# A graph layer's message stage: order written out by hand, more groups in flight, statistics by pairs of banks

## The chip, the core and the metric

The kernel runs on one core of one Trainium2 chip. The core's engines work side by side and meet through semaphores: PE (TensorE, the matrix unit, with its weight loads shown apart as PEld), DVE (VectorE), ACT (ScalarE), POOL (GpSimd) and SP (SyncE, which here only issues DMAs). PSUM, the memory that matmuls write to, has 8 banks of 512 floats in each of 128 partitions. The metric is the device time of one execution in microseconds (us). The time before is the median of three runs, 5669.56 us (5662.26 to 5670.88).

## The reference

One layer of a graph network over 12,500 nodes with 96 features and 412,500 edges, which come sorted by their destination `dst` and carry four attributes each:

```python
def _mlp(h, W, b, gamma, beta):
    h = relu(h @ W + b)
    return gamma * (h - mean(h, 0)) * rsqrt(var(h, 0) + EPS) + beta
node_feat = _mlp(x, W_node, ...)
edge_feat = _mlp(edge_attr, W_edge, ...)
message   = _mlp(concatenate([x[src], x[dst], edge_feat]), W_msg, ...)
out = layernorm(x + segment_sum(message, dst) + node_feat)
```

The normalisation in `_mlp` runs over all rows, so the edge part needs the statistics of relu(edge MLP) over all edges before a single message can be made, and the message part needs the statistics of all messages before the end.

## The kernel before, in words

**Tiling.** 128 edges make a tile, four tiles a *group* (`GT`, `GE` = 512 edges), four groups a *block* (`BG`). There are 806 groups in 202 blocks. Because edges are sorted by destination, a group touches a window of at most 30 nodes (`WN`), which begins at a node number held in `base`.

**Stage 1, tables (L136).** `p_tab` = x @ W_msg's first part (needed by source) and `q_tab` = x @ W_msg's second part (needed by destination) go to DRAM. `table()` fills PSUM tiles `pt` (4 buffers) and copies them out by ACT and DVE in turn.

**Stage 2, nodes (L202) and edge statistics (L234).** For each block `edge_norm()` runs three matmuls of 10 rows by 512 columns (L249) into a tile of three PSUM banks (two buffers), one relu on ACT over all three (L252, 128x1536) and three `bn_stats` on DVE (L254). From the result come `w_e`, the scaled edge weights, and `bias`.

**POOL beside it.** POOL gathers rows of `p_tab` by source with indirect DMAs, one per tile, four per group (L289). While stage 2 runs, it gathers the first 26 blocks (`SPILL`), here called *early*, into `stage` (two buffers); SP writes them to DRAM (`spill`, L303) and they are read back when their turn comes (`pb`, L404). After the early blocks POOL fills a ring of 30 groups (`RING`) with the groups that follow; from then on a group's slot must be freed before the next one is gathered. The order of SP and POOL up to here is written out by hand (`manual_schedule`).

**Stage 3, messages (L342 to L440).** The 176 other blocks, here called *late*, are taken in turn, with the 26 early ones spread evenly between them. For each block `load()` has SP fetch the edge attributes (L346), the window offsets (L347) and, after a load of four window bases to DVE's and SP's registers (L349), four windows of `q_tab` into `rhs` (L353, two slots). `prepare()` makes the four products `pr`, 6 rows by 512 columns each, into one tile of four banks (L362); ACT takes the relu of 96 rows of it (L364, 96x2048), DVE the zero test of the 30 others (L365, 30x2048), which is a one-hot of the destination in the window. Both make `left`. Then for each group `message()` runs four matmuls `z` = left x rhs (L371: edge part, destination part and bias together), DVE makes a second one-hot `h[.., 97:127]` (L373) and adds the gathered rows (`hs` = z + pg, L377), and ACT takes the relu into `h` (L378). One group later `reduce()` runs four matmuls `pa` = h transposed times [h | one-hot] (L386), and DVE adds them to the window of `agg` (L389, the segment sum) and to `gram` (L390, the messages' moments). `hs` is the last reader of a ring slot: POOL's gathers of the group 30 further on wait for it. In this stage the program's scheduler sets the order on each engine. PSUM: pr 4 banks, z 2 and pa 2.

**Stage 4, end (L598).** The messages' normalisation, a product per node tile, and the layer norm.


Of the kernel before, what the change touches and what calls it, by code (L numbers as in the profile page):

```python
# [22 lines left out]
P = 128  # L23
# [27 lines left out]
WN = 30  # L51
KR = C + WN + 1

SPILL = 26 * BG
RING = 30
J = 8


# [12 lines left out]
def gnn(ctx, tc, t):  # L71
# [61 lines left out]
        return s[:, 0:1], s[:, 1:2]  # L133


    def table(out, w, work, ps, queues):  # L136

        rows = out.rearrange("(p b) f -> p b f", b=NB)
        for c in range(0, NB, CH):
            r = work.tile([P, CH, C], F32, name="trow", bufs=3)  # L140
            for j, i in enumerate(range(0, CH, NBK)):
                n = min(NBK, CH - i)
                pt = ps.tile([P, NBK, C], F32, name="pt", bufs=4)
                for g in range(n):
                    k = COL[c + i + g]
                    nc.tensor.matmul(pt[:, g, :], xp[:, k:k + P], w, start=True, stop=True)  # L146
                if j % 2:
                    nc.scalar.activation(r[:, i:i + n, :], pt[:, :n, :], AF.Copy)  # L148
                else:
                    nc.vector.tensor_copy(r[:, i:i + n, :], pt[:, :n, :])  # L150
            queues[c // CH % len(queues)].dma_start(rows[:, c:c + CH, :], r)
            yield

    with tc.tile_pool(name="win_w", bufs=1) as work, tc.tile_pool(name="win_ps", bufs=2, space=PSUM) as ps:
        for _ in table(p_tab, w_msg[:, 0, :], work, ps, (nc.sync, nc.scalar)):
            pass

    nc.sync.dma_start(vec, t["vecs"])
# [75 lines left out]
    def edge_norm():  # L234

        with tc.tile_pool(name="es", bufs=2) as work, tc.tile_pool(name="es1", bufs=1) as one, \
                tc.tile_pool(name="es_ps", bufs=2, space=PSUM) as ps:
            stats = one.tile([P, NS, NBL, 6], F32, name="estats")
            for b in range(NBL):
                if b % J == 0:  # L240
                    yield
                    ea = work.tile([P, J, GE], F32, name="ea")
                    n = min(J, NBL - b)
                    for i in range(NS):
                        nc.sync.dma_start(ea[Q * i:Q * i + 2 * EK, :n, :],
                                          t["ea"][EK * i:EK * (i + 2), b:b + n, :])
                pr = ps.tile([P, NS, GE], F32, name="pr")
                for i in range(NS):
                    nc.tensor.matmul(pr[:, i, :], wide[Q * i:Q * i + 2 * EK, :],  # L249
                                     ea[Q * i:Q * i + 2 * EK, b % J, :], start=True, stop=True)  # L250
                r = work.tile([P, NS, GE], F32, name="r")
                nc.scalar.activation(r, pr, AF.Relu)  # L252
                for i in range(NS):
                    nc.vector.bn_stats(stats[:, i, b, :], r[:, i, :])  # L254

            part = one.tile([P, NS, 2], F32, name="part")
            square = one.tile([P, NS], F32, name="square")
# [27 lines left out]
    def fast(ring):  # L285
# [21 lines left out]
        store = blocks()  # L307
        with tc.manual_schedule(engines={ET.SP, ET.Pool}):
            with tc.tile_pool(name="tab_w", bufs=1) as work, tc.tile_pool(name="tab_ps", bufs=2, space=PSUM) as ps:
                for i, _ in enumerate(table(q_tab, w_msg[:, 1, :], work, ps, (nc.sync,))):  # L310
                    if i in (3, 6):
                        next(store)
            next(store)
# [9 lines left out]
                pass  # L323
            got = {g: ahead_of(g) for g in range(SPILL, SPILL + RING)}

        with tc.tile_pool(name="fix", bufs=1) as fix, tc.tile_pool(name="msg", bufs=2) as work, \
                tc.tile_pool(name="msg_ps", bufs=2, space=PSUM) as ps:
            gram = fix.tile([C + 1, C + 1], F32, name="gram")
            nc.vector.memset(gram, 0.0)
            rhs = fix.tile([P, 2, BG, C], F32, name="rhs")  # L330
            nc.vector.tensor_copy(rhs[:C], w_e[:, None, None, :].to_broadcast([C, 2, BG, C]))
            for i in range(2):
                for k in range(BG):
                    nc.sync.dma_start(rhs[KR - 1:KR, i, k, :], bias)
            left = [fix.tile([P, BG, GE], F32, name=f"left{i}") for i in range(2)]
            for x in left:
                nc.vector.memset(x[C:], 1.0)
            hb = [fix.tile([P, GT, P], F32, name=f"h{i}") for i in range(4)]
            for x in hb:
                nc.vector.memset(x[:, :, C:C + 1], 1.0)  # L340

            def load(s, b):  # L342

                n = min(BG, NG - b * BG)
                ea = work.tile([P, GE], F32, name="ea")
                nc.sync.dma_start(ea, t["eaq"][:, b, :])  # L346
                nc.sync.dma_start(ea[EK:P:Q, :], rel_d[:, b * BG * GE:(b + 1) * BG * GE]  # L347
                                  .rearrange("o (g e) -> (o g) e", g=BG))
                _, val = nc.values_load_multi_w_load_instructions(  # L349
                    base[:, b * BG:(b + 1) * BG], engines=[ET.DVE, ET.SP], min_val=0, max_val=N - 1,  # L350
                    skip_runtime_bounds_check_because="they are nodes' numbers")
                for i in range(n):
                    nc.sync.dma_start(rhs[C:C + WN, s % 2, i, :], q_tab[bass.ds(val[i], WN), :])  # L353
                return ea, val

            def prepare(s, b, ea):

                n = min(BG, NG - b * BG)
                x = left[s % 2]
                pr = ps.tile([C + WN, BG, GE], F32, name="pr", bufs=1)  # L360
                for i in range(n):
                    nc.tensor.matmul(pr[:, i, :], we[Q * i:Q * i + EK + 1, :],  # L362
                                     ea[Q * i:Q * i + EK + 1, :], start=True, stop=True)
                nc.scalar.activation(x[:C, :n, :], pr[:C, :n, :], AF.Relu)  # L364
                nc.vector.tensor_scalar(x[C:C + WN, :n, :], pr[C:, :n, :], 0.0, None, op0=OP.is_equal)  # L365

            def message(s, g, h, pg):
                n = min(GT, NT - g * GT)
                z = ps.tile([P, GT, C], F32, name="z")
                for i in range(n):  # L370
                    nc.tensor.matmul(z[:, i, :], left[s % 2][:KR, g % BG, i * P:(i + 1) * P],  # L371
                                     rhs[:KR, s % 2, g % BG, :], start=True, stop=True)
                nc.vector.tensor_tensor(  # L373
                    h[:, :, C + 1:C + 1 + WN], rel[:, g, :].unsqueeze(2).to_broadcast([P, GT, WN]),
                    iota[:, None, :].to_broadcast([P, GT, WN]), op=OP.is_equal)
# [1 line left out]
                nc.vector.tensor_add(hs[:, :n, :], z[:, :n, :], pg[:, :n, :])  # L377
                nc.scalar.activation(h[:, :n, :C], hs[:, :n, :], AF.Relu)  # L378

            def reduce(g, h, val):  # L380

                n = min(GT, NT - g * GT)
                pa = ps.tile([C + 1, P], F32, name="pa")
                for i in range(n):
                    r = min(P, E - (g * GT + i) * P)
                    nc.tensor.matmul(pa[:, :C + 1 + WN], h[:r, i, :C + 1], h[:r, i, :C + 1 + WN],  # L386
                                     start=i == 0, stop=i == n - 1)
                to = agg[:, bass.ds(val, WN)]
                nc.vector.tensor_tensor(to, pa[:, C + 1:C + 1 + WN], to, op=OP.add)  # L389
                nc.vector.tensor_add(gram, pa[:, :C + 1], gram)  # L390


            early, late = list(range(SPILL // BG)), list(range(SPILL // BG, NBL))
            order = []
            for i, b in enumerate(late):
                order.append(b)
                while early and (SPILL // BG - len(early)) * len(late) < i * (SPILL // BG):
                    order.append(early.pop(0))
            order += early

            def fetch(b):
                if b * BG < SPILL:
                    back = work.tile([P, BG, GT, C], F32, name="pb")
                    nc.sync.dma_start(back, spill[b].rearrange("p g (a c) -> p g a c", a=GT))  # L404
                    for i in range(BG):
                        got[b * BG + i] = back[:, i, :, :]

            ea, val = load(0, order[0])
            prepare(0, order[0], ea)
            fetch(order[0])  # L410
            last, n, ahead = None, 0, SPILL + RING
            for s, b in enumerate(order):
                more = s + 1 < len(order)
                if more:
                    ea, then = load(s + 1, order[s + 1])
                    fetch(order[s + 1])
                for g in range(b * BG, min((b + 1) * BG, NG)):
                    if g % BG == 1 and more:
                        prepare(s + 1, order[s + 1], ea)
                    h = hb[n % len(hb)]  # L420
                    n += 1
                    message(s, g, h, got.pop(g))
                    if last:
                        reduce(*last)
                    last = g, h, val[g % BG]
                    if g >= SPILL and ahead < NG:
                        got[ahead] = ahead_of(ahead)
                        ahead += 1
                val = then
            reduce(*last)  # L430

            d = fix.tile([C, C], F32, name="d")
            s = fix.tile([C, 3], F32, name="s")
# [234 lines left out]
```

## Time and profile before

| what | value |
|---|---|
| median of three runs | 5669.56 us |
| the profiled execution: its time, its span | 5713.74 us, 5712.0 us |
| mean granted TensorE clock in it | 0.656 of full speed |
| first and last `hs` (L377) in it | 1246 us, 5646.5 us |
| ring filled for the first time (POOL idle from there to 1247) | 1160 us |
| POOL's last gather begins at about | 5571 us |
| POOL gathers | 3223, of which 416 early ones |

The profile is one execution. A row of the groups reads: line, engine, operation, out<-in with shapes, count | busy us in all, mean ns of one | idle us of the engine just before these instructions, and what ended most of it ("issue" means nothing that the profile shows). A timeline row reads: start in us, duration in us, engine, line, operation, count of instructions merged, and in brackets the idle time before it and what ended that. A row of stretches gives each engine's busy us and count in a stretch of the span, and the granted clock as a share of full speed (PEclk). "x8" for four matmuls in f32 is right: each is recorded as two passes.

### The profile page before, as it was taken

The numbers are of one execution on the slowest core, as the hardware profiler recorded it, in microseconds if no ns is written. First come the engines' busy times: TensorE is split into PE (matmuls) and PEld (weight loads), VectorE is DVE, ScalarE is ACT, GpSimd is POOL, SyncE is SP. The second block draws the span as 40 slices with busy tenths as digits, with TensorE's granted clock in tenths as the row PEclk, the third lists the DMA queues.
The fourth block names the chain that finished last, engine by engine and source line by source line (L and its number), as shares of the span: only waits on it lengthen the run. The fifth ranks groups of instructions, "written<-read, shape, count | busy, mean of one in ns | idle before, by whom it ended". The sixth has DMA issues, their size and how long they took to land. (4 is left out here: it accounts for less than half of the span.)

```text
span 5712.0 us, 52958 instructions
## 1 busy us (share of the span) xinstructions
PE 3507.9 (61%) x16561; PEld 2613.4 (46%) x16561; DVE 1830.5 (32%) x4227; ACT 1126.2 (20%) x1304; POOL 3070.7 (54%) x3231
## 2 busy tenths in 40 slices
PE   3445666146666666766667566676566666665768
PEld 3331111024545455555555455455455555554547
DVE  1134555142323223232222232232322222322326
ACT  0113444021111111111111111111111111111113
POOL 2254444725555565555565555655555655556550
PEclk9955555557776666566666766666666666666667
DMA  3232323212222222222222222222222222222212
GB/s 117 73 97 56 70 63 68 47 42 51 52 52 49 46 50 52 50 52 49 52 46 51 50 51 49 47 52 49 51 50 52 46 50 52 49 52 46 50 44 82
DMA packets 190423, 315.48 MB, mean 55 GB/s; under 512 B 95817, under 2 KB 96201, under 8 KB 189128
## 3 DMA queue, kind: packets, MB, share of 16 engines
q0 software_dynamic: 103136, 158.62, 13.2%
q1 hardware_dynamic: 83502, 141.01, 8.9%
q10 hardware_dynamic: 3496, 12.36, 0.7%
q8 instruction: 137, 2.24, 0.2%
q14 instruction: 152, 1.25, 0.1%
HBM read 270.34 MB, written 41.37 MB: 55 GB/s over the span
## 5 line engine op out<-in xcount | busy, mean ns | idle before, releaser
L289 POOL DMA_INDIRECT pg<-p_tab,src x2807 | 2670.2, 951 | 1884.8 <-issue 787.5
L371 PE MATMUL z<-rhs,left 127*128 127x96 f32 x6446 | 1330.3, 350 | 706.3 <-issue 385.0
L371 PEld LDWEIGHTS z<-rhs,left 127*128 127x128 f32 x6446 | 1181.7, 261 | 1158.2 <-issue 684.0
L386 PE MATMUL pa<-h 128*97 128x127 f32 x6446 | 1236.4, 355 | 656.2 <-issue 351.7
L386 PEld LDWEIGHTS pa<-h 128*97 128x97 f32 x6446 | 1077.7, 230 | 719.8 <-issue 377.2
L378 ACT ACTIVATE h<-hs 128x384 f32<-128x384 f32 x806 | 419.5, 521 | 3094.3 <-DVE hs L377 1528.7
L389 DVE TENSOR_TENSOR agg<-pa,agg 97x30 f32 x806 | 150.4, 187 | 1978.1 <-PE z L371 752.6
L377 DVE TENSOR_TENSOR hs<-z,pg 128x384 f32<-128x384 f32 x702 | 390.2, 556 | 1054.7 <-issue 471.4
L289 POOL DMA_INDIRECT stage<-p_tab,src x416 | 399.6, 961 | 608.1 <-DMA spill<-stage 428.3
L362 PE MATMUL pr<-ea,we 6*126 6x512 f32 x1612 | 601.4, 841 | 157.4 <-issue 102.5
L249 PE MATMUL pr<-ea,wide 10*128 10x512 f32 x1212 | 406.6, 1107 | 409.2 <-ACT r L252 264.8
L254 DVE BATCH_NORM_STATS2 estats<-r 128x6 f32<-128x512 f32 x606 | 372.1, 680 | 442.6 <-ACT r L252 287.2
L364 ACT ACTIVATE left<-pr 96x2048 f32<-96x2048 f32 x202 | 376.3, 1863 | 549.9 <-remote 260.7
L365 DVE TENSOR_SCALAR left<-pr 30x2048 f32<-30x2048 f32 x202 | 462.9, 2292 | 43.8 <-ACT left L364 37.6
L249 PEld LDWEIGHTS pr<-ea,wide 10*128 10x128 f32 x1212 | 114.5, 307 | 700.0 <-ACT r L252 484.4
L252 ACT ACTIVATE r<-pr 128x1536 f32<-128x1536 f32 x202 | 292.2, 1451 | 592.9 <-remote 384.4
L362 PEld LDWEIGHTS pr<-ea,we 6*126 6x126 f32 x1612 | 150.6, 232 | 226.0 <-issue 150.3
L373 DVE TENSOR_TENSOR h<-rel,iota 128x120 f32<-128x120 f32 x806 | 204.9, 275 | 2.4 <-issue 0.4
L390 DVE TENSOR_TENSOR gram<-pa,gram 97x97 f32<-97x97 f32 x806 | 201.8, 250 | 0.3 <-DVE agg L389 0.3
L146 PE MATMUL pt<-w_msg,xp 96*128 96x96 f32 x392 | 85.6, 423 | 139.2 <-ACT trow L148 131.4
L146 PEld LDWEIGHTS pt<-w_msg,xp 96*128 96x128 f32 x392 | 84.1, 332 | 140.5 <-ACT trow L148 132.2
L223 PE MATMUL py<-center,xp 96*128 96x96 f32 x196 | 43.1, 423 | 60.5 <-DVE y0s L227 37.5
(95 smaller groups left out, 443.5 us busy)
## 6 DMA issues: line engine op xcount, KB each, us to landing
ea<-in_eaq SPq DMA_DIRECT2D x202, 256.0 KB
pg<-p_tab,src POOLq DMA_INDIRECT x2807
spill<-stage SPq DMA_DIRECT2D x26, 768.0 KB
pb<-spill SPq DMA_DIRECT2D x26, 768.0 KB
rhs<-q_tab SPq DMA_DIRECT2D x806, 11.2 KB
ea<-in_ea SPq DMA_DIRECT2D x75, 160.0 KB
stage<-p_tab,src POOLq DMA_INDIRECT x416
q_tab<-trow SPq DMA_DIRECT2D x7, 672.0 KB
```

The source lines that it names most:

```text
L249: nc.tensor.matmul(pr[:, i, :], wide[Q * i:Q * i + 2 * EK, :], ea[Q * i:Q * i + 2 * EK, b % J, :], start=True, stop=True)
L252: nc.scalar.activation(r, pr, AF.Relu)
L254: nc.vector.bn_stats(stats[:, i, b, :], r[:, i, :])
L289: nc.gpsimd.indirect_dma_start(out=pg[:, i, :], out_offset=None, in_=p_tab[:, :], in_offset=bass.IndirectOffsetOnAxis(ap=src[:, k:k + 1], ...
L362: nc.tensor.matmul(pr[:, i, :], we[Q * i:Q * i + EK + 1, :], ea[Q * i:Q * i + EK + 1, :], start=True, stop=True)
L364: nc.scalar.activation(x[:C, :n, :], pr[:C, :n, :], AF.Relu)
L365: nc.vector.tensor_scalar(x[C:C + WN, :n, :], pr[C:, :n, :], 0.0, None, op0=OP.is_equal)
L371: nc.tensor.matmul(z[:, i, :], left[s % 2][:KR, g % BG, i * P:(i + 1) * P], rhs[:KR, s % 2, g % BG, :], start=True, stop=True)
L373: nc.vector.tensor_tensor(h[:, :, C + 1:C + 1 + WN], rel[:, g, :].unsqueeze(2).to_broadcast([P, GT, WN]), iota[:, None, :].to_broadcast([P ...
L377: nc.vector.tensor_add(hs[:, :n, :], z[:, :n, :], pg[:, :n, :])
L378: nc.scalar.activation(h[:, :n, :C], hs[:, :n, :], AF.Relu)
L386: nc.tensor.matmul(pa[:, :C + 1 + WN], h[:r, i, :C + 1], h[:r, i, :C + 1 + WN], start=i == 0, stop=i == n - 1)
```

## The change

Five things change.

1. `SPILL` goes from 26 to 34 blocks: eight more blocks are gathered early, written out and read back.
2. The statistics take PSUM in pairs of banks (four buffers of two instead of two of three): 303 relus of 128x1024 instead of 202 of 128x1536; the matmuls and `bn_stats` are as many as before.
3. The message stage is cut to single groups and its order is written out by hand on all five engines. Step k issues, where they exist: the relu and zero test of group k+3, `z` of k+2, one-hot, `hs` and relu of k, `pa` of k-1, the product `pr` of k+5, the adds of k-3, then the gather into the freed slot. On each engine this is the order of its own instructions: PE runs z(k+2), pa(k-1), pr(k+5); ACT the relu of k+3, then that of k; DVE the zero test of k+3, one-hot and hs of k, the adds of k-3.
4. PSUM is split anew: pr two tiles of one bank, z three, pa three. `left` becomes 8 buffers of one group (before: 2 of four groups), `h` 6 buffers (4), `rhs` 3 slots (2), `ea` 3 (2). A block's loads are issued two blocks ahead instead of one. The 12 rows of `bias` in `rhs` were 8. The bases are loaded to SP's registers in `load` and to DVE's before a block's first add.
5. `table()` gets 8 PSUM buffers for `q_tab` (4 before; `p_tab` stays at 4).

```diff
-SPILL = 26 * BG
+SPILL = 34 * BG
 RING = 30
+LEAD, SKEW = 5, 3
+LB, HB, RB = 8, 6, 3
...
-                pt = ps.tile([P, NBK, C], F32, name="pt", bufs=4)
+                pt = ps.tile([P, NBK, C], F32, name="pt", bufs=bufs)
...
-                tc.tile_pool(name="es_ps", bufs=2, space=PSUM) as ps:
+                tc.tile_pool(name="es_ps", bufs=4, space=PSUM) as ps:
...
-                pr = ps.tile([P, NS, GE], F32, name="pr")
                 for i in range(NS):
-                    nc.tensor.matmul(pr[:, i, :], wide[Q * i:Q * i + 2 * EK, :],
+                    k = NS * b + i
+                    if k % 2 == 0:
+                        pr = ps.tile([P, 2, GE], F32, name="pr")
+                    nc.tensor.matmul(pr[:, k % 2, :], wide[Q * i:Q * i + 2 * EK, :],
                                      ea[Q * i:Q * i + 2 * EK, b % J, :], start=True, stop=True)
-                r = work.tile([P, NS, GE], F32, name="r")
-                nc.scalar.activation(r, pr, AF.Relu)
-                for i in range(NS):
-                    nc.vector.bn_stats(stats[:, i, b, :], r[:, i, :])
+                    if k % 2:
+                        r = work.tile([P, 2, GE], F32, name="r", bufs=4)
+                        nc.scalar.activation(r, pr, AF.Relu)
+                        for o in (1, 0):
+                            nc.vector.bn_stats(stats[:, (k - o) % NS, (k - o) // NS, :], r[:, 1 - o, :])
...
-                for i, _ in enumerate(table(q_tab, w_msg[:, 1, :], work, ps, (nc.sync,))):
+                for i, _ in enumerate(table(q_tab, w_msg[:, 1, :], work, ps, (nc.sync,), 8)):
...
-                tc.tile_pool(name="msg_ps", bufs=2, space=PSUM) as ps:
+                tc.tile_pool(name="msg_ps", bufs=3, space=PSUM) as ps:
...
-            left = [fix.tile([P, BG, GE], F32, name=f"left{i}") for i in range(2)]
+            left = [fix.tile([P, GE], F32, name=f"left{i}") for i in range(LB)]
...
-            hb = [fix.tile([P, GT, P], F32, name=f"h{i}") for i in range(4)]
+            hb = [fix.tile([P, GT, P], F32, name=f"h{i}") for i in range(HB)]
...
+            def edges(k):
+                s, g = steps[k]
+                prs[k] = ps.tile([C + WN, GE], F32, name="pr", bufs=2)
+                i = Q * (g % BG)
+                nc.tensor.matmul(prs[k], we[i:i + EK + 1, :], eas[s][i:i + EK + 1, :], start=True, stop=True)
+
+            def prepare(k):
+                pr, x = prs.pop(k), left[k % LB]
+                nc.scalar.activation(x[:C], pr[:C], AF.Relu)
+                nc.vector.tensor_scalar(x[C:C + WN], pr[C:], 0.0, None, op0=OP.is_equal)
+
+            def linear(k):
+                s, g = steps[k]
+                n = min(GT, NT - g * GT)
+                zs[k] = ps.tile([P, GT, C], F32, name="z")
                 for i in range(n):
-                    nc.tensor.matmul(z[:, i, :], left[s % 2][:KR, g % BG, i * P:(i + 1) * P],
-                                     rhs[:KR, s % 2, g % BG, :], start=True, stop=True)
+                    nc.tensor.matmul(zs[k][:, i, :], left[k % LB][:KR, i * P:(i + 1) * P],
+                                     rhs[:KR, s % RB, g % BG, :], start=True, stop=True)
...
+            with tc.manual_schedule(engines={ET.SP, ET.Pool, ET.PE, ET.DVE, ET.Activation}):
+                for k in range(-LEAD, n + SKEW):
+                    b = k + LEAD
+                    if b == 0:
+                        load(0)
+                        fetch(0)
+                        load(1)
+                    if 0 <= k < n and (k == 0 or steps[k][0] != steps[k - 1][0]):
+                        s = steps[k][0]
+                        if s + 2 < len(order):
+                            load(s + 2)
+                        if s + 1 < len(order):
+                            fetch(s + 1)
+                    if 0 <= k + LEAD - 2 < n:
+                        prepare(k + LEAD - 2)
+                    if 0 <= k + 2 < n:
+                        linear(k + 2)
+                    if 0 <= k < n:
+                        message(k)
+                    if 0 <= k - 1 < n:
+                        sums(k - 1)
+                    if k + LEAD < n:
+                        edges(k + LEAD)
+                    if k - SKEW >= 0:
+                        add(k - SKEW)
+                    if 0 <= k < n and steps[k][1] >= SPILL and ahead < NG:
+                        got[ahead] = ahead_of(ahead)
+                        ahead += 1
```

`message(k)` keeps its one-hot, `hs` and relu; `sums(k)` and `add(k)` are the two halves of the old `reduce()`.

## The prediction

> **What bounds the kernel now.** I read the page first: shares of busy time, the clock, the costly groups.
>
> ```profile
> PE 3507.9 (61%) x16561; PEld 2613.4 (46%) x16561; DVE 1830.5 (32%) x4227; ACT 1126.2 (20%) x1304; POOL 3070.7 (54%) x3231
> ...
> L289 POOL DMA_INDIRECT pg<-p_tab,src x2807 | 2670.2, 951 | 1884.8 <-issue 787.5
> L371 PE MATMUL z<-rhs,left 127*128 127x96 f32 x6446 | 1330.3, 350 | 706.3 <-issue 385.0
> ...
> L389 DVE TENSOR_TENSOR agg<-pa,agg 97x30 f32 x806 | 150.4, 187 | 1978.1 <-PE z L371 752.6
> ```
>
> No engine is full. The message stage lasts from 1246 to 5646.5 us (first and last hs) and 77% of the span; its longest queue is POOL's, 2687 gathers at 0.95 us with 0.30 us of issue between two, 1.25 x 2687 = 3359 us. What POOL waits for in the other thousand us is read from its own waits on the tile pg, between 1300 and 5400 us (duration, window, count of waits; then what ended them, with us and count):
>
> ```profile
> L289 POOL DMA_INDIRECT pg<-p_tab,src x2552: 941/947/1197, 1302.3 to 5398.8; - x197
>   issue: 711.5, 2260
>   DVE h L373: 553.5, 78
>   DVE gram L390: 294.8, 92
> ```
>
> With hs (84.5 us, 28 waits) that is some 198 waits of 4.75 us: a ring slot comes free when hs has read it. So DVE holds POOL, and DVE waits for PE. Why is PE late at 61%? The timeline of one burst answers it (start, duration, engine, in brackets the idle time before):
>
> ```profile
> 2619.15 2.01 PE L386 MATMUL pa<-h 128*97 128x127 f32 x8 [2.53 <-issue]
> 2621.09 2.08 PE L362 MATMUL pr<-ea,we 6*126 6x512 f32 x6
> ...
> 2625.02 0.32 PE L371 MATMUL z<-rhs,left 127*128 127x96 f32 x1 [0.90 <-issue]
> 2626.45 0.32 PE L371 MATMUL z<-rhs,left 127*128 127x96 f32 x1 [1.11 <-issue]
> 2626.57 0.94 POOL L289 DMA_INDIRECT pg<-p_tab,src  x1 [0.30 <-issue]
> ...
> 2630.73 0.19 DVE L389 TENSOR_TENSOR agg<-pa,agg 97x30 f32 x1 [11.87 <-PE z L371]
> 2631.44 0.56 DVE L377 TENSOR_TENSOR hs<-z,pg 128x384 f32<-128x384 f32 x1 [0.35 <-issue]
> ...
> 2632.26 1.20 POOL L289 DMA_INDIRECT pg<-p_tab,src  x1 [4.76 <-DVE h L373]
> ```
>
> While POOL gathers back to back, PE starts well and then crawls at one instruction per 1.1 to 1.4 us, waiting for nothing the profile names ("issue"); the DVE add has stood for 11.87 us for sums run at 2619. POOL runs out of slots at 2627.5, and about 3 us later everything is released at once: add 2630.73, hs 2631.44, next gather 2632.26. I call this the jam. The stretches give its price:
>
> ```profile
> core 0: us, PE busy (x) PEld busy (x) DVE busy (x) ACT busy (x) POOL busy (x), PEclk, DMA share, GB/s
> ...
> 1180.00:1205.00 25.00, 19.99 (x60) 6.22 (x60) 21.20 (x35) 17.19 (x12) 0.00 (x0) 0.50 0.10 36
> 2656.20:2680.60 24.40, 13.97 (x72) 11.52 (x72) 6.51 (x17) 3.74 (x5) 15.39 (x16) 0.64 0.21 46
> 2680.60:2691.20 10.60, 9.38 (x53) 8.53 (x54) 6.54 (x17) 3.74 (x5) 0.00 (x0) 0.68 0.25 65
> ```
>
> A late block (four groups, 16 gathers: 20 us, and one stop of 4.75) takes about 24.6 us, 6.15 per group; the early block after it, same work but no gathers, 10.6. The first row belongs to the statistics: PE is busy 80% of the time with 10-row matmuls, and the granted clock stays at 0.50.
>
> **The change part by part**, against the profiled execution (span 5712.0, its time 5713.74; the median of the runs is 0.9923 of that).
>
> **A. Eight more blocks early (26 to 34).** They leave the message stage as late blocks and come back as early ones: 8 x (24.6 - 10.6) = -112 us. Their 128 gathers go ahead of the ring in POOL's queue: 128 x 1.25 = +160. POOL stood idle from 1160 (ring full) to 1247 (first slot free), so 87 us of slack take part of it, but the statistics are themselves jammed while POOL gathers: an iteration of 12 PE instructions takes 16.8 us under gathers (ACT's relu at 1024.94 and again at 1041.74) and 1.86 us free, and after POOL stops PE needs 15 to 20 us to run freely (1160 to 1175-1180). So the front ends between +73 (all slack used) and about +145 later; I take +120, as the statistics' tail still comes behind POOL's end. A is +8; -40 to +33. SP writes 8 more blocks to DRAM and reads them back, 768 KB each; the reads lie a block ahead, beside 10 us of work at 65 GB/s: 0.
>
> **B. The written order: restart after a stop.** DVE's step now opens with the zero test of group k+3, which waits for ACT's relu of that group's product; hs, the one that frees the slot, is behind both. After the flush the path is relu of 96x512 (0.68, from the rows of L364 at 1.86 for 2048 and the 96x512 relu of the node stage at 0.68), zero test of 512 (0.70, from 2.29 for 2048 and 1.23 for 1024), one-hot 0.28, hs 0.56, POOL's release 0.26: 2.5 us where 2630.73 to 2632.26 shows 1.5. The adds that stood ahead of hs move three groups back (-0.4, counted in the 1.5). Behind the waiting zero test stand one-hot, hs and the adds of older groups, for hs POOL. So +1.0 to 1.1 us on some 200 stops: +220 at most; 0 if PE, which works meanwhile, gives it back later. No row shows such a return, but a late block's cycle is set mostly by POOL's 20 us; I take +50. More groups in flight may lengthen a burst; that is rival 1.
>
> **C. The written order: PE's clock.** Before, a block's four products pr (6 rows) ran together, x2 and x6, and z and pa ran in long dense rows. Now one pr of 512 columns stands alone between each four z and four pa. Warm, a group costs PE 0.89 (z, 2692.98) + 0.87 (pa, 2689.66) + 1.05 (pr, 2688.09) = 2.8 us; cold, about 1.8 + 1.94 + 2.06 (2906.34) = 5.8 us. From the row at 1180, a 6-row product like the 10-row ones does not raise the clock, and it fills 2.06 of 5.8 us, so that once cold a group is 64% dense: in the trace no stretch of 3.4 us with under 0.8 dense work is followed by the full clock. So the early blocks, where nothing but PE and the chain limits, take from 4 x 2.8 = 11.2 to 4 x 5.8 = 23.2 us instead of 10.6: 34 x (0.6 to 12.6) = +20 to +428. I take halfway, 17.2 us, +224, since a full clock once granted holds on through stretches at 0.8 busy, and some early blocks will begin warm. Late blocks: 23.2 us of cold PE work lie within a cycle of 24.7, but only where the jam lets them run: in B's bound.
>
> The Trainium skill ("TensorE: Matmul & The Clock Gate", the section on the HAM clock gate) has the clock rise after about 3.4 us of sustained matmul work and says nothing of narrow rows. By it the denser order would stay warm and C would be +20 instead of +224; the row at 1180 (80% busy, 0.50) speaks against that, and the measurement decides.
>
> **D. The rest, at nothing.** Statistics by pairs: 303 relus of 1024 at about 1.04 (between L252's 1.45 for 1536 and half of L364's 1.86) = 315 us instead of 293, on ACT that is idle for most of the stage; the count of matmuls (1212) and of bn_stats (606) stays; POOL's gathers set the pace, and without them bn_stats at 0.68 does: bounds -15 to +20. The q table with 8 buffers, 7 loops beside POOL's first gathers: -10 to 0. Four more bias DMAs at 0.6 us of SP issue, once: 0 to +3. DVE's own load of block bases moves from the block's load to its first add: same count. ACT issues 806 relus for 202: 806 x 0.68 = 548 for 376, at 20% busy; DVE goes from 1.84 to 1.97 us a group beside 5 or more.
>
> Sum: 8 + 50 + 224 = +282, 5996 profiled, x 0.9923 = **5950 us**. With every term low: -40 + 0 + 20 - 25 = -45, about 5625; every term high: 33 + 220 + 428 + 23 = +704, 6370.
>
> **Rivals.**
> 1. *Faster: longer bursts.* With z and pa three deep, eight left and six h, more groups' hs could be ready at a flush, so that POOL gathers more than four groups before it stops. The late group then costs 5.0 + 4.75/n instead of 6.19 (n = 4; measured 6.15). Against A + C = +232 on 640 groups it decides from n = 6 (0.40 x 640 = -253); n = 8 gives -380 + 232 = -148, 5520 us. For it: the flush at 2630.73 frees two hs in 1.1 us, as many as z had banks. Against: the jam starts some 9 us into a burst whatever is in flight, and DVE's order is now held by a relu and a zero test per group.
> 2. *Jam gone*: PE never falls behind, POOL sets the time: ring full at about 1350 (1160 + 160 + 30), 640 x 5.0 = 3200, 34 x 10.6 = 360, drain and end 145: 5055, 5016 us. Against: the statistics jam under gathers too, with quite another order.
> 3. *Slower still*: cold nearly everywhere and B in full: +430 to +704, 6100 to 6370. For it: mean clock already only 0.656.
> 4. *The change moves nothing*: the terms cancel, within 0.2% (11 us, about what a measurement of this kernel can tell): needs C near +20 and B near 0 at once.
>
> **How the numbers follow.** Forecast (+120 to +430, 5790 to 6100) 0.55; slower by 12 to 120 us 0.10; rival 3 0.12; rival 4 0.03; rival 1 0.15; rival 2 0.05. Faster 0.20, same 0.03, slower 0.77. Range 5520 to 6300: leaves out rival 2, about half of rival 1 and a third of rival 3, under 0.2; the forecast's own is 5790 to 6100.
>
> **What would show it.** A: last early gather and full ring later by about 160 us, first hs at 1350 to 1390; above 1400 the statistics cost more. B: the idle time before a burst's first gather 5.5 to 6 us instead of 4.75, its waits mostly ended by DVE's hs, and still about one stop per four groups; fewer than 110 stops would be rival 1. C: early blocks of 13 to 22 us and a mean clock under 0.62; 11 us and a clock above 0.68 would make C wrong. DVE's zero test should carry the long waits, ended by ACT. The prediction fails most likely if bursts grow beyond four groups.

## The result and the profile after

The changed kernel takes 5887.79 us (median; 5864.74 to 5895.30) against 5668.34 us before: a ratio of 1.0382, 95% interval [1.0351, 1.0413], 219 us slower. The forecast was 5950 us, 282 us slower. The profiled execution has a span of 5893.6 us (5712.0 before) and a mean clock of 0.648 (0.656). The execution profiled before took 5713.74 us, 0.8% more than the median of its runs, so the two traces differ by 182 us and not by 219.

The page of the changed kernel, engines and costly groups:

```profile
PE 4325.3 (73%) x16561; PEld 2924.7 (50%) x16561; DVE 1963.7 (33%) x4839; ACT 1213.1 (21%) x2009; POOL 3059.0 (52%) x3231
...
L294 POOL DMA_INDIRECT pg<-p_tab,src x2679 | 2540.3, 948 | 2031.5 <-DVE gram L435 1254.6
...
L393 DVE TENSOR_SCALAR left<-pr 30x512 f32<-30x512 f32 x806 | 561.5, 697 | 3232.7 <-ACT left L392 2422.3
...
L387 PE MATMUL pr<-ea,we 6*126 6x512 f32 x1612 | 1270.3, 875 | 146.9 <-issue 71.9
...
L434 DVE TENSOR_TENSOR agg<-pa,agg 97x30 f32 x806 | 144.1, 179 | 1.6 <-PE pa L422 1.6
```

The wait that stood before DVE's add (1978 us) now stands before the zero test, L393: 3233 us, put down to ACT, whose relu reads PE's product. PE is busy 817 us longer with the same count of instructions, and 669 us of that is the product pr (601 before, 1270 now): before, the four products of a block, on four different sets of rows, ran in about the time of two; now each stands alone.

POOL's waits on pg between 1300 and 5400 us:

```profile
L294 POOL DMA_INDIRECT pg<-p_tab,src x2380: 938/944/1935, 1299.7 to 5398.8; - x199
its engine sat idle before it (us, times) until:
  DVE gram L435: 1161.1, 169
  issue: 648.0, 2112
```

169 waits of 6.9 us, where there were 198 of 4.7 (the prediction's 4.75; these waits include the long ones over early blocks). `gram` is named because it starts 0.01 us after `hs` ends; the slot is freed by `hs`. One jam and its stop, in the timeline:

```profile
2619.59 1.12 PE L387 MATMUL pr<-ea,we 6*126 6x512 f32 x2
...
2630.82 0.94 POOL L294 DMA_INDIRECT pg<-p_tab,src  x1 [0.30 <-issue]
2631.16 0.32 PE L400 MATMUL z<-rhs,left 127*128 127x96 f32 x1 [1.56 <-issue]
...
2634.73 0.59 ACT L392 ACTIVATE left<-pr 96x512 f32<-96x512 f32 x1 [12.69 <-remote]
2635.36 0.70 DVE L393 TENSOR_SCALAR left<-pr 30x512 f32<-30x512 f32 x1 [13.67 <-ACT left L392]
2636.08 0.28 DVE L407 TENSOR_TENSOR h<-rel,iota 128x120 f32<-128x120 f32 x1
...
2636.40 0.56 DVE L411 TENSOR_TENSOR hs<-z,pg 128x384 f32<-128x384 f32 x1
...
2637.22 0.94 POOL L294 DMA_INDIRECT pg<-p_tab,src  x1 [5.46 <-DVE gram L435]
```

The product that PE ran at 2619.59 reaches ACT at 2634.73, 3 us after POOL's last gather ends (2631.76): the jam is as before. From there to POOL's next gather the path is the predicted one, relu, zero test, one-hot, hs: 2.49 us instead of 1.53.

An early block in three places, and the late block before the first of them, as stretches:

```profile
core 0: us, PE busy (x) PEld busy (x) DVE busy (x) ACT busy (x) POOL busy (x), PEclk, DMA share, GB/s
2689.40:2713.80 24.40, 16.79 (x74) 11.55 (x73) 7.20 (x20) 4.12 (x8) 15.10 (x17) 0.71 0.20 46
2713.80:2728.00 14.20, 14.20 (x67) 10.50 (x66) 7.20 (x20) 4.35 (x8) 2.19 (x3) 0.70 0.11 22
3395.10:3409.90 14.80, 14.80 (x47) 9.75 (x47) 7.23 (x21) 4.24 (x8) 0.00 (x0) 0.50 0.08 22
3532.50:3543.80 11.30, 11.30 (x67) 8.55 (x66) 7.25 (x21) 4.24 (x8) 2.18 (x3) 0.90 0.13 28
```

In an early block PE is busy without a gap, and the time goes by the clock: 11.3 us at 0.90, 14.8 at 0.50. Taking the time between the first hs of a block and that of the next, the 34 early blocks mean 14.1 us (10.6 before; correlation with the granted clock -0.77, before -0.01). Between 1400 and 5400 us, where POOL gathers, a late block that follows an early one means 22.8 (19.3 before), and the other late blocks 25.09 (25.04 before).

**POOL's ledger**, from the two traces, closes on the 182 us between the spans:

| | before | after | difference |
|---|---|---|---|
| first ring gather starts at | 1010 | 1151 | +141 |
| wait at the first full ring | 87 | 0 | -87 |
| ring gathers at 1.25 us | 2807 | 2679 | -160 |
| stops after 1400 us, in all | 974 in 202 | 1231 in 189 | +257 |
| of these, 2 to 8 us long (over no early block) | 161 of 3.66 | 149 of 5.11 | (+172) |
| longer ones, each over an early block | 24 of 14.8 | 31 of 14.8 | (+105) |
| shorter ones | 30 in 17 | 10 in 9 | (-20) |
| last gather to the end of the span | 149 | 172 | +23 |

That is +174; 8 us are in smaller pieces. The last gather starts at 5563 us before (not at 5571) and at 5722 after. The front is no loss. The stops are: +172 us in those that a burst of gathers between two late groups ends with, which are 1.45 us longer each. The stops over early blocks are as long as before, 14.8 us, although the early blocks themselves take 3.5 us more; there are only seven more of them, as eight more blocks are early. Below, stops of 2 to 8 us are counted up to 5550 us, which makes 142 of 5.10 in the changed kernel.

### The profile page after: what moved, and what is told of

The parts are those of the page before. It is cut to its first block, busy times and chain, and to the rows that moved or that the text cites. A ratio compares the mean times of both kernels' runs of the same rounds, so it can differ in the third digit from the quotient of the medians.

```text
span 5893.6 us, 53933 instructions
## 1 busy us (share of the span) xinstructions
PE 4325.3 (73%) x16561; PEld 2924.7 (50%) x16561; DVE 1963.7 (33%) x4839; ACT 1213.1 (21%) x2009; POOL 3059.0 (52%) x3231
## 3 DMA queue, kind: packets, MB, share of 16 engines
q0 software_dynamic: 103136, 158.62, 12.7%
## 5 line engine op out<-in xcount | busy, mean ns | idle before, releaser
L294 POOL DMA_INDIRECT pg<-p_tab,src x2679 | 2540.3, 948 | 2031.5 <-DVE gram L435 1254.6
L393 DVE TENSOR_SCALAR left<-pr 30x512 f32<-30x512 f32 x806 | 561.5, 697 | 3232.7 <-ACT left L392 2422.3
L422 PE MATMUL pa<-h 128*97 128x127 f32 x6446 | 1330.5, 362 | 375.5 <-issue 374.6
L387 PE MATMUL pr<-ea,we 6*126 6x512 f32 x1612 | 1270.3, 875 | 146.9 <-issue 71.9
L422 PEld LDWEIGHTS pa<-h 128*97 128x97 f32 x6446 | 1137.4, 236 | 475.7 <-issue 475.3
L392 ACT ACTIVATE left<-pr 96x512 f32<-96x512 f32 x806 | 471.1, 585 | 2488.8 <-remote 1697.8
L294 POOL DMA_INDIRECT stage<-p_tab,src x544 | 517.8, 952 | 631.3 <-DMA spill<-stage 412.5
L387 PEld LDWEIGHTS pr<-ea,we 6*126 6x126 f32 x1612 | 322.6, 247 | 343.2 <-issue 226.9
L253 PEld LDWEIGHTS pr<-ea,wide 10*128 10x128 f32 x1212 | 199.5, 322 | 445.4 <-issue 243.7
L257 ACT ACTIVATE r<-pr 128x1024 f32<-128x1024 f32 x303 | 294.1, 1024 | 431.5 <-remote 237.6
```

Of the source, the lines that this page charges most:

```text
L253: nc.tensor.matmul(pr[:, k % 2, :], wide[Q * i:Q * i + 2 * EK, :], ea[Q * i:Q * i + 2 * EK, b % J, :], start=True, stop=True)
L294: nc.gpsimd.indirect_dma_start(out=pg[:, i, :], out_offset=None, in_=p_tab[:, :], in_offset=bass.IndirectOffsetOnAxis(ap=src[:, k:k + 1], ...
L387: nc.tensor.matmul(prs[k], we[i:i + EK + 1, :], eas[s][i:i + EK + 1, :], start=True, stop=True)
L392: nc.scalar.activation(x[:C], pr[:C], AF.Relu)
L393: nc.vector.tensor_scalar(x[C:C + WN], pr[C:], 0.0, None, op0=OP.is_equal)
L422: nc.tensor.matmul(pas[k][:, :C + 1 + WN], h[:r, i, :C + 1], h[:r, i, :C + 1 + WN], start=i == 0, stop=i == n - 1)
```

## The experiments

The kernel before ran beside each (medians 5667 to 5733 us from chip to chip), so ratios are compared, and a ratio is turned into us with 5668.

**1. The parts apart.** Four kernels.

```diff
 e1_pairs, on before: statistics by pairs of banks, 4 PSUM buffers (nothing else)
 e2_spill34, on before:
-SPILL = 26 * BG
+SPILL = 34 * BG
 e3_front, on before: e1 and e2 and 8 buffers for q_tab
 e4_msg, on after: the new message stage with
-SPILL = 34 * BG
+SPILL = 26 * BG
 and the old statistics and q_tab buffers
```

> The kernel before with the new statistics alone (relus of two banks, four PSUM buffers); 26 early blocks, message stage as before. Theory, from the two traces: in the changed kernel the statistics end at 1039 us instead of 1205 although POOL gathers as long as before, because four buffers let PE use each of POOL's pauses further; so here the first hs comes at about 1080 to 1110, the 87 us in which POOL stood with a full ring (1160 to 1247) go, and the time falls by 60 to 90 us, to 5580 to 5610. Rival, the prediction's part D: POOL's early gathers set the front, the statistics' end does not matter, change within 15 us.

> The kernel before with 34 early blocks alone (old statistics, old message stage). The prediction's part A: the front ends 73 to 145 us later, the message stage is 112 us shorter, -40 to +33 us in all (5630 to 5700), statistics still ending behind POOL's early gathers. Rival: the eight blocks move only gathers that POOL has to make anyhow, and use the slack at the full ring: -50 us or more.

> All of the change but the message stage: 34 early blocks, new statistics, 8 buffers for the q table; message stage as before. Theory: POOL's idle time falls by 87 at the full ring, and 8 stops of about 4 us become early blocks of 10.6 (+53): -40 to -60 us against before, 5605 to 5630. If the front were what made the changed kernel slow, this would be slower than before. The rest of the change, the message order, then has to cost +260 to +280.

> The new message stage alone (26 early blocks, old statistics). Theory, by POOL's idle time in the changed kernel's trace: early blocks 14.1 us instead of 10.6 (26 x 3.5 = +91), a late block's stop 4.5 instead of 4.0 us (176 x 0.54 = +95), the 30 groups after the last gather 106 us instead of 77 (+29): +215, about 5880. Rival: the written order is harmless, and the loss comes from its meeting 34 early blocks and a ring that is not yet full when the stage begins: within 60 us of before.

| | ratio to before | interval | us |
|---|---|---|---|
| e1_pairs | 0.9927 | [0.9907, 0.9946] | -41 |
| e2_spill34 | 0.9998 | [0.9989, 1.0008] | -1 |
| e3_front | 0.9916 | [0.9899, 0.9932] | -48 |
| e4_msg | 1.0436 | [1.0409, 1.0464] | +247 |

The message stage alone makes the kernel slower, by more than all of the change does; the front gives 48 us back; the two nearly add up (0.9916 x 1.0436 = 1.035, measured 1.038). The statistics by pairs give 41 us in e1, where I had expected 60 to 90, and the eight early blocks nothing by themselves. The theory of e1 failed in its step too: the 87 us at the full ring do not go. First the kernel before, then e1:

```profile
1246.65 0.95 POOL L289 DMA_INDIRECT pg<-p_tab,src  x1 [87.27 <-DVE hs L377]
```

```profile
1215.52 0.95 POOL L292 DMA_INDIRECT pg<-p_tab,src  x1 [85.95 <-DVE hs L380]
```

What e1 gains is that the whole front runs some 30 us sooner: the first ring gather starts at 980 instead of 1010, as POOL's waits for the stage buffer fall from 428 to 400 us, and the first hs comes at 1215 instead of 1246. It is in e2, with eight more early blocks and nothing else, that the wait at the full ring goes; POOL's ledger of e2 closes at about 0 (first ring gather +202, wait at the full ring -87 and waits after it up to 1400 us -29, 128 gathers -160, stops after 1400 us +66, end +9). The last `bn_stats` shows how the two work on the front, here in the kernel before, e1, e2 and e3:

```profile
L254 DVE BATCH_NORM_STATS2 estats<-r x606: 674/676/697, 403.8 to 1205.1; 128x6 f32<-128x512 f32 x152
```

```profile
L257 DVE BATCH_NORM_STATS2 estats<-r x606: 634/678/698, 402.7 to 1179.4; 128x6 f32<-128x512 f32 x152
```

```profile
L254 DVE BATCH_NORM_STATS2 estats<-r x606: 674/676/697, 403.9 to 1114.3; 128x6 f32<-128x512 f32 x152
```

```profile
L257 DVE BATCH_NORM_STATS2 estats<-r x606: 674/678/697, 393.5 to 1057.6; 128x6 f32<-128x512 f32 x152
```

With eight more early blocks the *old* statistics end 91 us sooner. The traces suggest why: early gathers are broken by waits for the stage buffer (412 us in 14 waits in the changed kernel) in which the statistics run freely, while the 120 gathers that fill the ring run unbroken, and before, from 1010 to 1160, they lay over the statistics' end. That reading was not tested by itself.

**2. The chain after a stop, the clock, and a pause.** Four kernels.

```diff
 e5_hsfirst, on after
-                    if 0 <= k + LEAD - 2 < n:
-                        prepare(k + LEAD - 2)
-                    if 0 <= k + 2 < n:
-                        linear(k + 2)
                     if 0 <= k < n:
                         message(k)
+                    if 0 <= k + LEAD - 2 < n:
+                        prepare(k + LEAD - 2)
+                    if 0 <= k + 2 < n:
+                        linear(k + 2)
 e6_fullrows, on after; we is [P, BG, C + WN], zero outside each group's 6 rows
-                nc.tensor.matmul(prs[k], we[i:i + EK + 1, :], eas[s][i:i + EK + 1, :], start=True, stop=True)
+                nc.tensor.matmul(prs[k], we[:, g % BG, :], eas[s], start=True, stop=True)
 e7_before_full, on before: the same in L362
 e8_pause, on after
                         got[ahead] = ahead_of(ahead)
                         ahead += 1
+                        nc.gpsimd.memset(pause, 0.0)
```

> The changed kernel with one thing swapped: in each step the one-hot, hs and relu of group k come before the relu and zero test of group k+3, on DVE and ACT. Tests part B. Theory: after a stop hs no longer stands behind a relu (0.58) and a zero test (0.70), so POOL's first gather comes about 1.2 us sooner after PE's results arrive (2609.61 to 2612.10 in the changed kernel, 2.5 us, becomes 1.2 to 1.5). If the whole chain lies on the path, the time falls by 1.0 to 1.2 us on some 165 stops, 165 to 200 us; if PE gives most of it back, as the stops of 4.5 us per late block instead of 4.0 suggest, by 60 to 100 us. Rival: PE's clock alone makes the loss, change within 20 us.

> The changed kernel with the products pr made over all 128 rows: the weights of each of the four groups are zero outside its own 6 rows, so results, counts and columns are the same. Tests part C. Theory: what keeps the clock at 0.5 is the narrow product, 6 rows of 128; with full rows the clock in the message stage rises from 0.67 towards 1.0 wherever PE is busy, an early block falls from 14.1 to 11 or 12 us and the last 30 groups from 106 to about 85: 34 x 2.5 + 25 = -110 us at least, and more if the late blocks gain as well. Rival: the clock counts busy time whatever the rows, and the early blocks are slow by the order of the engines: change within 20 us, clock still 0.65.

> The same full-row products in the kernel before. Theory: its early blocks (10.6 us at PE 89% busy) hardly gain; its late blocks are set by POOL and the jam: 0 to -60 us, clock above 0.70. If PE's clock were what sets the late blocks, more than -150 us.

> The changed kernel with a memset of 128x512 on POOL, about half a us, after the four gathers of each group. Tests what the jam needs. One theory: it is the unbroken run of gathers that holds up PE's completions, and a short pause lets them through; then no stop of 5 us per four groups is left, and a late block takes 4 x 5.5 = 22 to 23 us instead of 24.5: -150 to -250 us. Rival: the jam goes by the share of time in which POOL gathers, or needs some 3 us of silence as at each stop's end; then the pauses come on top: +100 to +350 us (at most 640 x 0.55), with stops as before.

| | ratio to before | interval | against the changed kernel, us | clock | early block | other late block, 1400 to 5400 us | stops of 2 to 8 us |
|---|---|---|---|---|---|---|---|
| after | 1.0382 | [1.0351, 1.0413] | | 0.648 | 14.1 | 25.09 | 142 of 5.10 |
| e5_hsfirst | 1.0068 | [1.0051, 1.0085] | -178 | 0.656 | 15.05 | 23.90 | 152 of 3.85 |
| e6_fullrows | 1.0197 | [1.0178, 1.0215] | -105 | 0.704 | 11.4 | 24.83 | 133 of 5.14 |
| e8_pause | 1.0229 | [1.0206, 1.0251] | -87 | 0.646 | 15.3 | 23.93 | 100 of 4.20 |
| e7_before_full | 0.9997 | [0.9984, 1.0010] | | 0.735 | 10.5 | 24.71 | |

*e5*: the swap is worth the whole chain, 178 us where 165 to 200 were expected. Where hs heads DVE's queue at the end of a jam, POOL follows in 0.83 us:

```profile
2606.66 0.56 DVE L411 TENSOR_TENSOR hs<-z,pg 128x384 f32<-128x384 f32 x1 [5.83 <-PE pr L387]
...
2607.49 0.94 POOL L294 DMA_INDIRECT pg<-p_tab,src  x1 [3.76 <-DVE hs L411]
```

The stops are of two kinds here: 84 without a zero test ahead of hs in DVE's run, 3.30 us, and 68 with one, 4.54. In the changed kernel all 142 have it, in the kernel before 7 of 161 at most. (A run is a row of DVE instructions with little idle time between them. How little is a matter of choice, and moves the counts of the two kinds by some 20 and their lengths by up to 0.6 us.)

*e6*: the same columns, instructions and results with 128 rows instead of 6; an early block, as a stretch:

```profile
core 0: us, PE busy (x) PEld busy (x) DVE busy (x) ACT busy (x) POOL busy (x), PEclk, DMA share, GB/s
3501.99:3512.86 10.87, 10.87 (x75) 8.95 (x75) 7.20 (x21) 4.02 (x8) 2.18 (x3) 0.96 0.18 43
```

The clock was held down by the narrow rows and not by PE's gaps: PE is as busy as in the changed kernel's early blocks, and the clock is 0.96 where it was 0.50 to 0.90. The record of the clock says it for the whole message stage. It changes in steps of 3.41 us; of the steps at half clock in which PE was busy for 99% or more, 428 of 564 were followed by another at half clock in the changed kernel, and 13 of 135 with full rows. In POOL's ledger the 105 us are 13 fewer stops of 2 to 8 us (-62), stops over early blocks of 13.8 us instead of 14.8 (-31) and a shorter end (-12); the length of the former stays, at 5.14. In the kernel before (e7) the clock rises more, from 0.656 to 0.735, and the time does not move: its other late blocks fall by 0.3 us, from 25.04 to 24.71. Four products that ran side by side now run one after the other there (903 us of PE in all instead of 601), so this run does not tell whether the late blocks of before need no faster PE or whether the two effects cancel.

*e8*: 0.55 us of memset after every group, 0.41 of it on top of POOL's 0.30 between gathers, makes the kernel faster, by 87 us where 150 to 250 less or 100 to 350 more were expected. The jam comes all the same (stops of 4.2 us from gather to gather, the memset included), but there are 100 of them instead of 142, because the bursts are longer: 94 of 133 have 20 gathers or more, where the changed kernel has 2 of 189.

**3. Together.**

```diff
 c1_both = e5 and e6
 c2_pause = c1 and e8's memset
 e9_front_pause = e3 (message stage as before) and e8's memset
```

> The changed kernel with both: hs ahead of the relu and zero test, and the products over all 128 rows. If the chain after a stop (ratio 1.0382 to 1.0068) and the clock (1.0382 to 1.0197) are separate costs, they add: 1.038 - 0.031 - 0.018 = 0.989 of before, faster than before and about the same as the kernel with all of the change but the message stage (0.9916). If they overlap (a warm PE makes the chain shorter, or the chain hides the clock), 1.000 to 1.005.

> The same with the half-us memset on POOL after each group's gathers. In the changed kernel the pause gave -87 us (1.0382 to 1.0229) although it adds 0.41 us to each of 640 groups: a late block fell from 24.5 to 23.5. If it works by letting PE's completions through, it adds to the other two: 0.975 to 0.980. If it only did what the earlier hs does (more done before PE falls behind), it brings nothing here or costs up to 0.41 x 640 = 260 us: 0.99 to 1.03.

> The kernel with all of the change but the message stage (0.9916 of before), with the same pause on POOL. If the pause lets PE's completions through whatever the order of the message stage, -60 to -150 us: 0.965 to 0.98. If it helps only an order that is late to release the slot, 0 to +260 us: 0.99 to 1.035.

| | ratio to before | interval | early block | stops with a zero test ahead | without |
|---|---|---|---|---|---|
| c1_both | 1.0083 | [1.0055, 1.0112] | 12.2 | 87 of 4.81 | 49 of 3.45 |
| c2_pause | 0.9873 | [0.9851, 0.9894] | 13.45 | 49 of 4.38 | 75 of 3.02 |
| e9_front_pause | 0.9906 | [0.9890, 0.9923] | 12.7 | | |

The two gains do not add: c1 is no faster than e5 alone, against my expectation of 0.989. The early blocks gain (12.2 us against 15.05), but the stops get longer again: in all, those of 2 to 8 us hold POOL as long as in e5 (593 us against 591 after 1400 us), fewer and longer. In c1's timeline, at the end of a jam, the zero test of the step before heads the queue although hs(k) now precedes the zero test of its own step:

```profile
2619.19 0.59 ACT L392 ACTIVATE left<-pr 96x512 f32<-96x512 f32 x1 [8.71 <-remote]
2619.81 0.70 DVE L393 TENSOR_SCALAR left<-pr 30x512 f32<-30x512 f32 x1 [9.96 <-ACT left L392]
...
2621.00 0.55 DVE L411 TENSOR_TENSOR hs<-z,pg 128x384 f32<-128x384 f32 x1
...
2621.82 0.94 POOL L295 DMA_INDIRECT pg<-p_tab,src  x1 [4.83 <-DVE hs L411]
```

The zero test of k+3 needs pr(k+3), which PE runs *after* z(k). So DVE can pass hs(k) and be caught by the jam at the zero test, and hs(k+1) stands behind it. With full rows it is caught there 87 times in 136, with narrow ones 68 in 152. The pause takes 2.1% off c1, less than the 0.975 to 0.980 I expected, and does nothing to the message stage of before (0.9906 against 0.9916).

**4. Nothing ahead of hs.** If that is the cause, it goes when all that stands between hs(k) and hs(k+1) needs only results that PE makes before z(k): once hs(k) has run, DVE can then be held at hs(k+1) alone. In c1 the zero test of k+3 breaks this; below, pr(k+2) is made before z(k).

```diff
 d1_head, on c2_pause
-LEAD, SKEW = 5, 3
+LEAD, SKEW = 4, 3
...
+                    if 0 <= k + 2 < n:
+                        prepare(k + 2)          (the relu alone)
                     if 0 <= k < n:
                         message(k)
-                    if 0 <= k + LEAD - 2 < n:
-                        prepare(k + LEAD - 2)
-                    if 0 <= k + 2 < n:
-                        linear(k + 2)
+                    if 0 <= k + 2 < n:
+                        zero_test(k + 2)
                     if 0 <= k - 1 < n:
                         sums(k - 1)
                     if k + LEAD < n:
                         edges(k + LEAD)
+                    if 0 <= k + 2 < n:
+                        linear(k + 2)
```

> The kernel with hs first, full rows and pause (0.9873), with the steps shifted so that at a stop nothing can stand ahead of hs on DVE: zero test and relu of group k+2 instead of k+3, pr of k+4, and PE's order pa, pr, z, so that all that DVE and ACT do before hs(k+1) needs only results that PE makes before z(k+1). Theory: what decides the stop is the instruction at the head of DVE's queue when PE's completions come. Stops of 2 to 8 us with a zero test ahead of hs last 4.4 us (49 of them) to 5.1 (all 142 in the changed kernel), without one 3.0 to 3.4. Here no stop has a zero test ahead, stops are 3.0 to 3.3 us, and 49 x 1.36 = 67 us go: 0.973 to 0.978. Rival: with one group less in preparation PE waits for the zero test each time, early blocks get longer than 13.5 us and eat the gain: 0.985 to 1.01.

5526.28 us, a ratio of 0.9654 [0.9630, 0.9678]: 3.5% faster than before and 7% faster than the changed kernel. POOL's waits on pg from 1300 to 5400 us, to be held against 1161 us above:

```profile
L295 POOL DMA_INDIRECT pg<-p_tab,src x2576: 940/944/1795, 1299.8 to 5366.3; - x199
its engine sat idle before it (us, times) until:
  issue: 679.4, 2406
  DVE hs L415: 567.5, 155
```

A jam still holds DVE for 10 us, but it now ends with hs, and POOL follows 0.83 us after:

```profile
2613.50 0.56 DVE L415 TENSOR_TENSOR hs<-z,pg 128x384 f32<-128x384 f32 x1 [9.68 <-remote]
2614.09 0.70 DVE L397 TENSOR_SCALAR left<-pr 30x512 f32<-30x512 f32 x1
...
2614.33 0.95 POOL L295 DMA_INDIRECT pg<-p_tab,src  x1 [2.50 <-DVE hs L415]
```

118 stops last 3.02 us with no zero test ahead; 16 have one somewhere in DVE's run (5.93 us), and these are stops over early blocks. The gain, 2.2% or 125 us over c2_pause, is twice the 67 us forecast from the stops. In the two traces the stops over no early block fall from 123 of 3.52 to 118 of 3.02 us, 76 us in all, and those over an early block from 32 of 10.6 to 32 of 8.4, 70 us. The second part goes with the early blocks, which fell from 13.45 to 11.4 us (34 x 2.05 = 70) where the rival had them get longer; I had not foreseen it. What in the new order does that was not taken apart, and the order was not run without the pause.

## Why the prediction was right, and where not

The direction, the place (message stage, not front) and the two mechanisms hold, and the time lies in the range; the likeliest time was 62 us too high. That it came so near is luck: terms of the sum were wrong by more than 100 us, in opposite directions. By its steps:

- **The jam** is there in the changed kernel (in the stop shown above all is released 3 us after the last gather), and stops remain in every kernel run; rival 2 (jam gone) fell. The prediction's 4.75 us a stop is a mean over two kinds: 3.66 us between late groups, 14.8 over early blocks.
- **A**, +8 forecast: e2 alone gives -1. Right as a sum, wrong inside. The early gathers end 141 us later (160 forecast; 202 in e2, with the old statistics), but the first hs came at 1157 us (1218 in e2), not at 1350 to 1390: the step "the statistics' tail still comes behind POOL's end" failed. They end at 1039 (1115 in e2), ahead of POOL's last early gather (1150; 1211 in e2), and messages need only the first groups of the ring, not a full one.
- **D**, statistics by pairs at nothing, bounds -15 to +20: measured -41 in e1. The step "POOL's gathers set the pace" failed: with the statistics by pairs the early gathers themselves end 30 us sooner, for POOL waits less for the stage buffer (400 us instead of 428), and the first hs comes 31 us sooner. Why those waits shorten was not tested. With A it is -48 (e3) instead of +8.
- **B**, +50 taken, 0 to 220 as bounds: the path was right to 0.1 us (2.49 measured, 2.5 forecast), its weight was not. "A late block's cycle is set mostly by POOL's 20 us" was the wrong ground for so little: POOL stands still in the whole of the chain, and PE gave hardly anything back. e5 returns 178 us; the stops of 2 to 8 us show +1.44 each. Beside the kernel before, the other late blocks grew by only 0.05 us, because the rest of the new order, as e5 suggests, is worth about -1.1 (23.90 against 25.04): the chain ate that gain.
- **C**, +224 taken, 20 to 428: 105 us by e6. The early blocks grew by 34 x 3.5 = 119, but that is no second measurement: POOL's stops over them did not grow, and most of e6's 105 us are fewer stops of 2 to 8 us. After the last gather come +23, which the forecast left out. The mechanism is right (clock against rows, full rows), the size half. The early block at a clock of 0.50 takes 14.8 us, not 23.2: PE runs 47 matmul records in it instead of the 72 of a block, so a third of the work lies outside it.
- **Rival 1**, longer bursts, fell as it was put: of 189 bursts 123 have 16 gathers and two have 20; six groups were never reached. e5 is no different (one burst of 20). Bursts of five and six groups came only with the pause: in e8, 94 of 133 have 20 gathers or more, and 21 of these 24 or more.
- **The signs**: waits of 5.5 to 6 us instead of 4.75 (6.9, counted in the same way; 5.10 without those over early blocks), early blocks of 13 to 22 (14.1), zero test with the long waits ended by ACT (yes), clock under 0.62 (0.648, wrong).

So the sum came near because C was too high by about 120 us and A with D by 56, and B too low by 130: -48 + 178 + 105 = 235, against 219 measured. Even this sum is no proof, since its parts are not separate: with both costs taken out (c1, 1.0083) the kernel is still 95 us slower than the one with the message stage of before (e3, 0.9916). The chain and the clock together return 169 us, not 283. What makes up the 95 us is not shown; d1, with 76 us less in the stops over no early block, speaks for the zero test that still stands between two hs as a part of it.

The Trainium skill ("TensorE: Matmul & The Clock Gate", the section on the HAM clock gate) takes the clock by PE's busy time. Here PE was busy for 100% of the early blocks of the changed kernel and for 98% of those of e6, and the clock was 0.70 in the one and 0.88 in the other on the mean; only the rows of pr differ. So busy time alone does not settle the clock here.

## What to carry to other kernels

When an engine hands out slots that another waits for, look at what stands at the head of its queue at the moment when the stall ends, not at its busy time: all that is held by the stall together with the releasing instruction, and stands ahead of it, is paid at every stop (here 2.49 us from the relu that ended the jam to POOL's next gather, and 0.83 where hs ended it). Order each queue so that what stands between one releasing instruction and the next needs no newer result than the first of the two did. A deeper pipeline can gain per group and still lose, when the work for later groups is put in front of it.

## What the runs showed of the hardware

- While POOL gathers without a break, PE's results reached other engines at a fixed pace per instruction in the statistics stage: a relu each 11.20 us in e1 for 8 PE instructions (1000.87, 1012.07, 1023.27), each 16.8 us for 12 before; 1.40 us per instruction in both.
- Matmuls over 6 of 128 rows keep the granted clock low though PE is busy: 0.648 against 0.704 for the span, 0.70 against 0.88 in early blocks, with nothing else changed. Of the steps of 3.41 us at half clock in which PE was busy for 99% or more, 428 of 564 led to another at half clock with the narrow rows, 13 of 135 with the full ones.
- Small products on different sets of rows overlap: four took about the time of two (601 us of PE in all against 1270).
- A memset of 0.55 us on POOL after each four gathers made two kernels faster by 1.5 and 2.1% and left a third as it was (0.9906 against 0.9916). In e8 the bursts of gathers grew from mostly 16 to mostly 20 and the stops fell from 142 to 100; why stays open.
